# A recurrent kernel on one core: joining copies moved, one filling unit moved, and the last group of steps projected plainly

## The chip, the cores and the metric

The kernel runs on one core of a Trainium2 chip. Its engines are named as in the profile: PE (matrix products), PEld (PE's weight loads), DVE (vector), ACT (scalar, activations and copies), POOL (the general engine) and SP (which here issues DMAs). The metric is the device time of one execution in microseconds; three runs of the kernel before have a median of 1363.82 us (1363.69 to 1363.88).

## The reference

A gated recurrent unit runs over T=128 steps for a batch of 64, with D=H=512, all in 32-bit floats. The output is x plus the sequence of states.

```python
comb = concat([x_t, h]);  z = sigmoid(comb @ Wz + bz);  r = sigmoid(comb @ Wr + br)
h_cand = tanh(concat([x_t, r * h]) @ Wh + bh)
h_new = (1 - z) * h + z * h_cand                  # what is put out, added to x
h_next = tanh(h_new @ Wp + bp) if prop else h_new # prop: every fourth step but the last
```

## The kernel before, in words

**Layout.** The 64 rows of the batch and two halves of the 512 columns make 128 partitions, so h is 128x256. A gate's product (`product`, L196) is four parts k, each two matmuls, one per half (`products`, L184), with 64 columns of stationary operand and 256 of moving one. Every matmul in 32-bit floats is two records in the profile, so a gate is 16 records.

**A step** (the loop from L569) has, in PE's order: the r product with `wh[R]`; the z product; two half turns of rh (`turn`, L205: each is four bf16 transposes on PE and a copy, to `rhT`); the candidate's product, `rc<-wh,rhT`; two half turns of h, the first copied by DVE, the second by ACT; in a step with propagation, also the product with `wp` and two half turns of its tanh. Around it ACT runs the sigmoids of r (L601), the seed of r, the sigmoids of z (L616, L617), the seed of z, tanh (L647) and the seed of the candidate; DVE runs the products and sums (L602, L618, L648, L653). `ORDER` is the order k=0, 2, 1, 3: the first two need only the first half turn.

**The part that comes from x** is worked out ahead, for groups of four steps. The first two groups use `plain` (L411): 12 units of 256 columns a step, with the bias added by DVE into `cp`. From group 2 on, `batches` (L483) does two groups at once by a two-level scheme with seven instead of eight products at each level: 98 units of 192 columns for eight steps. It needs differences of weights, some of them stored in place in `wx` (L316, L324), sums of x made by POOL (`sum_raw12` and so on), and recombinations by POOL into `cp` (`outer_...`). `seed` (L392) copies from `cp` into PSUM what the next step's products add to.

**What sets the order.** Nothing is scheduled by a planner: each engine runs its queue in the order of the program text. The units wait in `queue`; `fill(n)` (L400) puts the next n of them at a place in a step; the copies that read a finished batch (its ends) wait in `pending` until the next `read_out()`. `PLACES` (L537) has, for u = (t-3) mod 8, how many units lie ahead of the candidate, how many behind it, and how many in the propagation. The second number is split over L656, L661 and L663: of 6 units four lie ahead of the first turn of h, one between the turns and one behind the second. The queue for groups 30 and 31 is filled at t=114 and used up in t=122.

**x turned.** From group 4 on POOL splits x in words (`words_x`), a transposing DMA on SP's queue (`planes_x`) turns it, and `join_x` (L268) puts the two planes together on ACT: two copies of 128x512 words in each of the steps with u=5, 6 (even groups) and u=1, 3 (odd ones). They stand at L638, behind the candidate's product and ahead of tanh in ACT's order.

Of the kernel before, what the change touches and what calls it, by code (L numbers as in the profile page):

```python
# [17 lines left out]
def kernel(  # L18
# [29 lines left out]
    nc = tc.nc  # L48
    B, T, D = x.shape
# [6 lines left out]
    Q4 = 4  # L56
    CHUNK = 4
    FIRST = 2
    R, Z, H_ = range(3)
    assert B * S == P and D == H and T % 8 == 0  # L60

# [115 lines left out]
    def idle(n):  # L177
        for _ in range(n):
            nc.tensor.matmul(  # L179
                scratch[0][:B, :], lhsT=zeros[:, :B], rhs=zeros, start=True, stop=True  # L180
            )
# [14 lines left out]
    def product(ps, lT, w, k, start=False):  # L196
        s0, c0 = divmod(k, C)
        products(ps, lT[:, c0, ts(s0, B)], lambda s: w[:, k, ts(s, N)], start)
# [69 lines left out]
    def join_x(g, i):  # L268

        if g * Q4 >= T:  # L270
            return
        new_xT(g)
        nc.scalar.copy(
            xT[g][:, i].bitcast(U16).rearrange("p c (n w) -> p w c n", w=2), xv[g][:, i]
        )
# [62 lines left out]
    def sum_raw12(g):  # L338
        v = xT[g]
        sx[g, 12] = one.tile([P, 4, C, B], F32, tag="s12r", name=f"s12r_{g}")  # L340
        four([sx[g, 12][:, n] for n in range(4)], v[:, 0], v[:, 1])
# [6 lines left out]
    def sum_s12(g):  # L348
        v = xT[g]
        o = sx[g, "o12"] = one.tile([P, 2, 2, P], F32, tag="o12", name=f"o12_{g}")  # L350
        nc.gpsimd.tensor_add(o[:, 0], v[:, 2:4, 0, :], v[:, 2:4, 1, :])
        nc.gpsimd.tensor_sub(o[:, 1], o[:, 0], v[:, 0:2, 0, :])
        s = sx[g, 56] = one.tile([P, 4, 2, B], F32, tag="s56", name=f"s56_{g}")
        four([s[:, n] for n in range(4)], o[:, :, 0], o[:, :, 1])
# [37 lines left out]
    def seed(i, t):  # L392
        if t < T:
            nc.scalar.copy(cut(slots[i]), G[t][:, :, i, :])  # L394
# [5 lines left out]
    def fill(n):  # L400
        for _ in range(min(n, len(queue))):
            unit, end = queue.pop(0)
            unit()
            if end is not None:
                pending.append(end)
# [5 lines left out]
    def plain(t):  # L411
# [20 lines left out]
        ]  # L432
        return [(u, None) for u in units[:-1]] + [(units[-1], end)]

    MB = {}

    def batch(n, ms):

        def region(ps, m):
            return ps[:, m].rearrange("p g u -> p (g u)")  # L440

        def unit(ps, m, j, start):
            g, i = ms[m]
            products(
                region(ps, m), lhs(g, i, j), lambda s: factor(i, j)[:, s], start and m == 0
            )

        def units(ps, j, start):
            return [lambda m=m: unit(ps, m, j, start) for m in range(2)]

        def blocks():
            return MB[n].rearrange("p m b g (a u) -> p m b a g u", a=2)

        def end_1():
            MB[n] = mbp.tile([P, 2, 2, 3, P], F32, tag="mb", name=f"mb_{ms[0][0]}_{ms[0][1]}")
            for m, (g, i) in enumerate(ms):
                M[g, i] = MB[n][:, m]
            T2[n] = one.tile([P, 2, 3, P // 2], F32, tag="cx", name=f"cx_{ms[0][0]}_{ms[0][1]}")
            q1 = one.tile([P, 2, 3, P // 2], F32, tag="cq", name=f"cq_{ms[0][0]}_{ms[0][1]}")
            nc.scalar.copy(T2[n], x_ps)  # L460
            nc.scalar.copy(q1, q_ps)
            nc.vector.tensor_add(T2[n], r_ps, T2[n])  # L462
            nc.vector.tensor_add(blocks()[:, :, 0, 0], a_ps, q1)

        def end_2():
            q2 = one.tile([P, 2, 3, P // 2], F32, tag="cq", name=f"cq2_{ms[0][0]}_{ms[0][1]}")
            nc.scalar.copy(q2, q_ps)  # L467
            nc.vector.tensor_add(blocks()[:, :, 0, 1], r_ps, q2)  # L468
            nc.vector.tensor_add(blocks()[:, :, 1, 0], x_ps, q2)
            nc.vector.tensor_add(blocks()[:, :, 1, 1], q_ps, T2[n])  # L470

        free = units(a_ps, 2, True)
        one_ = units(q_ps, 1, True) + units(r_ps, 5, True) + units(x_ps, 7, True)
        two_ = units(x_ps, 4, False) + units(q_ps, 6, False) + units(r_ps, 3, False)
        seq = [(u, None) for u in free + one_ + two_]
        seq[7] = (seq[7][0], end_1)
        seq[13] = (seq[13][0], end_2)
        return seq

    M = {}  # L480
# [2 lines left out]
    def batches(g):  # L483

        if g * Q4 >= T:
            return []
        ms = [(g, i) for i in (1, 2, 6, 5, 7, 3, 4)] + [(g + 1, i) for i in (1, 6, 2, 5, 3, 7, 4)]
        return sum((batch((g, n), ms[2 * n : 2 * n + 2]) for n in range(7)), [])


    def flat(v):
# [47 lines left out]
    )  # L539


    idle(10)
    spread(0, rc)
    turn_x(0, nc.vector)
# [24 lines left out]
    for t in range(T):  # L569
# [7 lines left out]
        if t < 3:  # L577
            queue.extend(plain(2 * t + 2) + plain(2 * t + 3))
            places = (12, 12)
        elif t == 3:  # L580
            queue.extend(batches(FIRST))
            places = (8, 8, 6)
        elif u == 7:

            queue.extend(batches(even + 2))


        for k in ORDER:
# [1 line left out]
        if t < 6:  # L590
            turn_x((2, 5, 8, 11, 13, 15)[t])
        read_out()
        if u == 0 and pair >= 1:
            outer_u2(odd - 2)
        if t == 3:
            sum_s12(FIRST)
# [3 lines left out]
        for c in range(C):  # L600
            nc.scalar.activation(act_ps[c], slots[R][:, ts(c, P)], AF.Sigmoid)  # L601
            nc.vector.tensor_mul(rh[:, ts(c, P)], act_ps[c], h[:, ts(c, P)])  # L602
        seed(R, t + 1)


        for k in ORDER[: 2 if last else K]:
            product(slots[Z], hT, wh[Z], k)
        rhT = new_T("rhT", f"rhT_{t}")
        for c in range(C):
            turn(rh, rhT, c, f"rhT_{t}", nc.vector)  # L610
        if last:
            for k in ORDER[2:]:
                product(slots[Z], hT, wh[Z], k)
        z = two.tile([P, N], F32, tag="z", name=f"z_{t}")
        keep = two.tile([P, N], F32, tag="keep", name=f"keep_{t}")
        nc.scalar.activation(z, slots[Z], AF.Sigmoid)  # L616
        nc.scalar.activation(slots[Z], slots[Z], AF.Sigmoid, scale=-1.0)  # L617
        nc.vector.tensor_mul(keep, slots[Z], h)  # L618
        seed(Z, t + 1)
        if prop:  # L620
            nc.scalar.copy(cut(slot_p), bias[:, :, 3, :])
# [2 lines left out]
        if t == 0:  # L624
            sum_outer()
            for i in (6, 7, 4):
                sum_inner(i, nc.gpsimd)
                sum_inner_1(i, nc.gpsimd)
        fill(places[0])
        if t < 3:  # L630
            turn_x((3, 6, 9)[t])

# [2 lines left out]
            product(slots[H_], rhT, wh[H_], k)  # L635
        if t != 2:
            read_out()
        if pair >= 0:  # L638
            for n in range(2):
                if u in (5, 6):  # L640
                    join_x(even + 2, 2 * (u - 5) + n)
                elif u in (1, 3) and pair >= 1:
                    join_x(odd, u - 1 + n)
        h_new = two.tile([P, N], F32, tag="h", name=f"h_{t}")
        for c in range(C):
            pc = act_ps[c]
# [4 lines left out]
                nc.vector.tensor_add(o, pc, o)  # L651
                continue
            nc.vector.tensor_add(h_new[:, ts(c, P)], pc, keep[:, ts(c, P)])  # L653
        seed(H_, t + 1)
        read_out()
        fill(places[1] - 3 if places[1] > 6 else 4)  # L656
        h = h_new
        if not last:
            hT = new_T("hT", f"hT_{t}")
            turn(h, hT, 0, f"hT_{t}", nc.vector)  # L660
            fill(1)  # L661
            turn(h, hT, 1, f"hT_{t}", nc.scalar)
        fill(2 if places[1] > 6 else 1)  # L663
        if t == 2:
            sum_outer_1()
        if t == 3:
# [2 lines left out]
        if prop:  # L669
            for k in ORDER:  # L670
                product(slot_p, hT, wp, k)
            read_out()
            h = two.tile([P, N], F32, tag="hprop", name=f"hprop_{t}")
            for c in range(C):
                nc.scalar.activation(h[:, ts(c, P)], slot_p[:, ts(c, P)], AF.Tanh)
            fill(places[2] - 2)
            hT = new_T("hT", f"hpT_{t}")
            for c in range(C):
                turn(h, hT, c, f"hpT_{t}", (nc.vector, nc.scalar)[c])
            fill(2)  # L680
        if t < 5:
            turn_x((4, 7, 10, 12, 14)[t])


        if pair >= 0:
            if u == 0 and pair >= 1:
                outer_c22(odd - 2)
                outer_c21(odd - 2)
            if here:
                if u == 0:  # L690
                    sum_s34(even)
                    outer_1(even)
                elif u == 1:
                    outer_c11(even)
                    sum_raw12(odd)
                elif u == 2:
                    outer_u1(even)
                    outer_5(even)
                    sum_raw4(even)
                elif u == 3:  # L700
                    outer_c12(even)
                    outer_u2(even)
                    outer_c22(even)
                    sum_s12(odd)
                elif u == 4:
                    outer_c21(even)
                    outer_1(odd)
                    sum_s34(odd)
                elif u == 5:
                    outer_u1(odd)  # L710
                    outer_c11(odd)
                    sum_raw4(odd)
                elif u == 7:
                    outer_5(odd)
                    outer_c12(odd)
        if u == 7 and pair >= -1 and (even + 2) * Q4 < T:
# [12 lines left out]
            nc.gpsimd.tensor_add(xr[g][:, j, :], xr[g][:, j, :], h_new)  # L729


        n = 0
        if t >= T - CHUNK:
            n = {T - 2: 3, T - 1: 1}.get(t, 0)
# [60 lines left out]
```

## Time and profile before

| | us |
|---|---|
| median of three runs | 1363.82 |
| profiled execution | 1362.82 |
| its span, first to last instruction | 1361.0 |
| PE busy | 1341.8 |
| POOL busy | 935.7 |
| DVE busy | 686.0 |
| ACT busy | 630.6 |
| from the r product of t=118 (starts 1264.12) to the end | 96.88 |
| from the r product of t=123 (starts 1313.52) to the end | 47.48 |

All rows but the first are from one execution. The granted clock of PE was 0.998 over the span. Ends of matmuls in the trace are modelled, and the two halves of a product overlap, so a sum of busy times says less than the distances between starts. A row of the order in time has its start, its length, the engine, the line, the operation, what it writes and reads, sizes and count; in brackets stands how long the engine sat idle before it, and what ended that. All values of u and t in this document are those of the loop.

### The profile page before, as it was taken

Reading aid. Unit: us, or ns where it says so; the run is one execution under the profiler, and the core shown is the slowest. Engines: PE = TensorE matmul, PEld = TensorE weight load, DVE = VectorE, ACT = ScalarE, POOL = GpSimd, SP = SyncE. Lnnn points to the kernel's source line nnn. Section 1 sums busy time; section 2 is a strip of 40 time slices with the busy share of each in tenths; the row PEclk is TensorE's granted clock in tenths of the full one; section 3 lists DMA queues with packets and bytes.
Section 4 is the critical chain, followed back from the end, with each engine's and each line's share of the span. In section 5 each row is a group of like instructions: output and inputs, shape, how many; then the busy total and the mean of one; then the engine's idle time right before and its main releaser. Section 6 shows DMA issues by size and latency. Waiting matters only on the chain.

```text
span 1361.0 us, 37468 instructions
## 1 busy us (share of the span) xinstructions
PE 1341.8 (99%) x15348; PEld 1033.1 (76%) x15348; DVE 686.0 (50%) x1875; ACT 630.6 (46%) x1857; POOL 935.7 (69%) x1140
## 2 busy tenths in 40 slices
PE   9999999999999999999999999999999999999996
PEld 6877777777777777777777777777777777777764
DVE  3255555555555555555555555555554555555543
ACT  1234544444544544444445444545445445444443
POOL 3448776778667768676787767777676686767740
PEclk9999999999999999999999999999999999999999
DMA  9011223121221222213222221222212212131010
GB/s 287 13 33 34 62 49 78 32 58 39 64 63 33 63 48 48 64 33 78 49 45 52 63 64 33 63 36 60 63 32 64 59 37 63 41 71 33 17 33 16
DMA packets 113572, 73.86 MB, mean 54 GB/s; under 512 B 61556, under 2 KB 109812, under 8 KB 113400
## 3 DMA queue, kind: packets, MB, share of 16 engines
q1 hardware_dynamic: 112336, 69.68, 22.6%
q8 instruction: 121, 1.98, 0.6%
q10 hardware_dynamic: 1064, 1.78, 0.4%
q14 instruction: 51, 0.42, 0.1%
HBM read 39.99 MB, written 16.78 MB: 42 GB/s over the span
## 4 chain that ended last, share of the span: by engine, by line
PE 98%; DVE 1%; ACT 0%; issue 0%; POOL 0%; DVEq 0%; POOLq 0%; ACTq 0%
PE rc L187 33%; PE zp L187 20%; PE scratch_q L187 11%; PE scratch_x L187 11%; PE scratch_r L187 10%; PE scratch_a L187 6%; PE turn L212 6%; PE scratch_q L179 0%; DVE h L653 0%; DVE turn L648 0%; ACT z L616 0%; PE rc L160 0%; ACT turn L647 0%; ACT xT L203 0%; ACT zp L617 0%
## 5 line engine op out<-in xcount | busy, mean ns | idle before, releaser
L187 PE MATMUL rc<-wh,rhT 128*64 128x256 f32 x2048 | 246.6, 381 | 2.0 <-ACT zp L617 2.0
L495 POOL TENSOR_TENSOR cp<-mb,mb 128x768 f32<-128x768 f32 x75 | 136.4, 1819 | 112.8 <-ACT rc L394 67.6
L187 PEld LDWEIGHTS rc<-wh,rhT 128*64 128x64 f32 x2048 | 158.9, 137 | 54.5 <-ACT zp L617 12.4
L187 PE MATMUL rc<-wh,hT 128*64 128x256 f32 x1536 | 183.1, 380 | 0.5 <-DVE hT L203 0.2
L187 PE MATMUL zp<-wh,hT 128*64 128x256 f32 x1536 | 183.2, 379 | 0.0
L203 DVE COPY rhT<-turn 128x256 uint16<-128x256 uint16 x256 | 96.7, 420 | 126.1 <-PE turn L212 126.1
L495 POOL TENSOR_TENSOR cp<-mb 128x768 f32<-128x768 f32 x45 | 81.9, 1819 | 108.2 <-ACT rc L394 107.0
L648 DVE TENSOR_TENSOR turn<-turn,z 128x128 f32<-128x128 f32 x256 | 75.5, 295 | 159.7 <-ACT turn L647 159.7
L187 PEld LDWEIGHTS zp<-wh,hT 128*64 128x64 f32 x1536 | 117.5, 137 | 47.3
L729 POOL TENSOR_TENSOR xr<-xr,h 128x256 f32<-128x256 f32 x127 | 92.8, 731 | 86.2 <-DVE h L653 85.2
L187 PEld LDWEIGHTS rc<-wh,hT 128*64 128x64 f32 x1536 | 111.6, 137 | 44.9 <-issue 1.0
L601 ACT ACTIVATE turn<-rc 128x128 f32<-128x128 f32 x256 | 55.4, 261 | 155.3 <-issue 84.2
L462 DVE TENSOR_TENSOR cx<-scratch_r,cx 128x384 f32<-128x384 f32 x105 | 58.6, 558 | 128.3 <-ACT cx L460 128.3
L203 ACT COPY hT<-turn 128x256 uint16<-128x256 uint16 x127 | 47.3, 373 | 155.8 <-PE turn L212 96.6
L495 POOL TENSOR_TENSOR mb<-mb,mb 128x768 f32<-128x768 f32 x60 | 109.4, 1824 | 14.2 <-DVE mb L470 14.2
L468 DVE TENSOR_TENSOR mb<-scratch_r,cq 128x384 f32<-128x384 f32 x105 | 58.6, 558 | 91.0 <-ACT cq L467 91.0
L394 ACT COPY rc<-cp 128x256 f32<-128x256 f32 x254 | 95.6, 376 | 11.6 <-POOL s L335 0.4
L616 ACT ACTIVATE z<-zp 128x256 f32<-128x256 f32 x128 | 49.2, 384 | 102.7 <-PE zp L187 100.8
L647 ACT ACTIVATE turn<-rc 128x128 f32<-128x128 f32 x256 | 56.7, 261 | 76.2 <-PE rc L187 76.2
L212 PEld LDWEIGHTS <-h 128*64 128x64 bf16 x1016 | 47.7, 109 | 50.5 <-DVE h L653 45.7
L394 ACT COPY zp<-cp 128x256 f32<-128x256 f32 x127 | 47.8, 377 | 74.5 <-DVE keep L618 74.5
L212 PE MATMUL turn<-ident,h 128*64 128x128 bf16 x1016 | 76.7, 227 | 5.4 <-DVE h L653 5.4
(152 smaller groups left out, 2960.4 us busy)
## 6 DMA issues: line engine op xcount, KB each, us to landing
xr<-in_x_dram SPq DMA_DIRECT2D x62, 256.0 KB, 4.2
out_dram<-xr SPq DMA_DIRECT2D x62, 256.0 KB, 3.4
xs<-in_x_dram SPq DMA_DIRECT2D x56, 256.0 KB, 4.3
wh<-in_L_cond_Wr_dram SPq DMA_DIRECT2D x2, 512.0 KB, 7.5
wh<-in_L_cond_Wz_dram SPq DMA_DIRECT2D x2, 512.0 KB, 8.9
wh<-in_L_cond_Wh_dram SPq DMA_DIRECT2D x2, 512.0 KB, 11.4
early<-in_x_dram SPq DMA_DIRECT2D x4, 256.0 KB, 13.4
wp<-in_L_cond_Wp_dram SPq DMA_DIRECT2D x1, 1024.0 KB
```

Source lines behind the costliest of these rows:

```text
L187: nc.tensor.matmul(ps[s * B : (s + 1) * B], lhsT=lhs, rhs=rhs(s), start=start, stop=True, skip_group_check=True,)
L203: (eng.copy if eng is nc.scalar else eng.tensor_copy)(dst, src)
L212: nc.tensor.transpose(pt[s * B : (s + 1) * B, w, :], words.rearrange("p (n w) -> p w n", w=2)[:, w, :], ident16,)
L394: nc.scalar.copy(cut(slots[i]), G[t][:, :, i, :])
L462: nc.vector.tensor_add(T2[n], r_ps, T2[n])
L468: nc.vector.tensor_add(blocks()[:, :, 0, 1], r_ps, q2)
L495: nc.gpsimd.tensor_add(dst, a, b)
L601: nc.scalar.activation(act_ps[c], slots[R][:, ts(c, P)], AF.Sigmoid)
L616: nc.scalar.activation(z, slots[Z], AF.Sigmoid)
L647: nc.scalar.activation(pc, slots[H_][:, ts(c, P)], AF.Tanh)
L648: nc.vector.tensor_mul(pc, pc, z[:, ts(c, P)])
L729: nc.gpsimd.tensor_add(xr[g][:, j, :], xr[g][:, j, :], h_new)
```

## The change

- The two joining copies of a step are issued one behind the seed of r and one behind the sigmoids of z and `keep`, ahead of the seed of z.
- Where six units lie behind the candidate, four lie ahead of the first turn of h, two between the turns and none behind the second. Where eight lie there, the split stays five, one and two. In the first three steps (twelve) it is five, one, six instead of nine, one, two.
- The last group (31) is projected plainly. The queue filled at t=114 has only the 49 units of group 30; seven are left for t=118. At t=118 nine DMAs on SP's queue load k=1, 0 and 2 of `wx` again (k=3 was never changed in place). `plain_last` puts 48 units of 256 columns into the queue at t=119: the three gates of k=3 for t=124 and 125 first, then the rest.
- The last nine steps are thin: no units ahead of the candidate; z's product is split, two parts before the first half turn of rh, one after each; `TAIL` gives the units ahead of, between and behind the turns of h, and in the propagation. The seed of the candidate for the last step moves into that step.

```diff
+    def plain_last():
...
+        t0 = LAST * Q4
+        seq = [(u, None) for t in (t0, t0 + 1) for u in units(t, (R, Z, H_), (3,))]
+        for t in (t0, t0 + 1):
+            us = units(t, (R, Z, H_), (1, 0, 2))
+            seq += [(u, None) for u in us[:-1]] + [(us[-1], lambda t=t: end(t, (R, Z, H_)))]
+        for t, gates in ((t0 + 2, (R, Z, H_)), (t0 + 3, (R, Z)), (t0 + 3, (H_,))):
+            us = units(t, gates, (3, 1, 0, 2))
+            seq += [(u, None) for u in us[:-1]] + [(us[-1], lambda t=t, g=gates: end(t, g))]
+        return seq
...
+    def reload():
...
+        for k in (1, 0, 2):
+            for i in range(3):
+                load_w(wx[:, :, i, :], gates_in[i], k, k + 1, nc.sync)
...
+    TAIL = (
+        ((4, 1, 0), (2, 1)), ((4, 1, 0), ()), ((4, 1, 0), ()), ((4, 1, 0), ()),
+        ((4, 1, 0), (2, 1)), ((4, 1, 0), ()), ((5, 1, 2), ()), ((3, 1, 0), ()), ((0, 0, 0), ()),
+    )
...
+        thin = t >= T - 9
+        if thin:
...
+            places, behind = TAIL[t - (T - 9)]
+            if t == T - 9:
+                assert not queue
+                queue.extend(plain_last())
+        if t == T - 10:
...
+            places = (4, 6)
...
+        def join(n):
+            if pair >= 0 and u in (5, 6):
+                join_x(even + 2, 2 * (u - 5) + n)
+            elif pair >= 1 and u in (1, 3):
+                join_x(odd, u - 1 + n)
...
         seed(R, t + 1)
-
-
-        for k in ORDER[: 2 if last else K]:
+        join(0)
+
+
+        for k in ORDER[: 2 if thin else K]:
             product(slots[Z], hT, wh[Z], k)
...
             turn(rh, rhT, c, f"rhT_{t}", nc.vector)
-        if last:
-            for k in ORDER[2:]:
-                product(slots[Z], hT, wh[Z], k)
+            if thin:
+                product(slots[Z], hT, wh[Z], ORDER[2 + c])
...
         nc.vector.tensor_mul(keep, slots[Z], h)
+        join(1)
         seed(Z, t + 1)
...
-        fill(places[0])
+        if not thin:
+            fill(places[0])
...
-        fill(places[1] - 3 if places[1] > 6 else 4)
+        fill(places[0] if thin else 5 if places[1] > 6 else 4)
...
-            fill(1)
+            fill(places[1] if thin else 1 if places[1] > 6 else 2)
             turn(h, hT, 1, f"hT_{t}", nc.scalar)
-        fill(2 if places[1] > 6 else 1)
+        fill(places[2] if thin else places[1] - 6)
```

More of the change, by code (lines that the diff above doesn't have):

```diff
@@ L58 @@
     FIRST = 2
+    LAST = T // Q4 - 1
     R, Z, H_ = range(3)
@@ L433, in plain, with units, end @@
         return [(u, None) for u in units[:-1]] + [(units[-1], end)]
+    def plain_last():
+        def units(t, gates, first_k):
+            first, second = scratch[:2] if t % 2 == 0 else scratch[2:]
+            regions = (first[:, :N], first[:, N:], second[:, :N])
+            return [
+                lambda e=e, k=k: product(
+                    regions[e], xT[LAST][:, t % Q4], wx[:, :, e, :], k, k == 3 and e != Z
+                )
+                for k in first_k
+                for e in gates
+            ]
+        def end(t, gates):
+            first, second = scratch[:2] if t % 2 == 0 else scratch[2:]
+            new_cp(t // 2)
+            if R in gates:
+                nc.vector.tensor_add(
+                    G[t][:, :, 0:2, :],
+                    first.rearrange("p (g c n) -> p c g n", g=2, c=C),
+                    bias[:, :, 0:2, :],
+                )
+            if H_ in gates:
+                nc.vector.tensor_add(
+                    G[t][:, :, 2, :], cut(second[:, :N]), bias[:, :, 2, :]
+                )
+        t0 = LAST * Q4
[11 more added lines that the diff above has]
+                load_w(wx[:, :, i, :], gates_in[i], k, k + 1, nc.sync)
     MB = {}
@@ L448, in units @@
         def units(ps, j, start):
-            return [lambda m=m: unit(ps, m, j, start) for m in range(2)]
+            return [lambda m=m: unit(ps, m, j, start) for m in range(len(ms))]
         def blocks():
@@ L457, in end_1 @@
                 M[g, i] = MB[n][:, m]
+            nm = len(ms)
             T2[n] = one.tile([P, 2, 3, P // 2], F32, tag="cx", name=f"cx_{ms[0][0]}_{ms[0][1]}")
             q1 = one.tile([P, 2, 3, P // 2], F32, tag="cq", name=f"cq_{ms[0][0]}_{ms[0][1]}")
[L460 to L463, printed above, removed]
+            nc.scalar.copy(T2[n][:, :nm], x_ps[:, :nm])
+            nc.scalar.copy(q1[:, :nm], q_ps[:, :nm])
+            nc.vector.tensor_add(T2[n][:, :nm], r_ps[:, :nm], T2[n][:, :nm])
+            nc.vector.tensor_add(blocks()[:, :nm, 0, 0], a_ps[:, :nm], q1[:, :nm])
         def end_2():
             q2 = one.tile([P, 2, 3, P // 2], F32, tag="cq", name=f"cq2_{ms[0][0]}_{ms[0][1]}")
[L467 to L470, printed above, removed]
+            nm = len(ms)
+            nc.scalar.copy(q2[:, :nm], q_ps[:, :nm])
+            nc.vector.tensor_add(blocks()[:, :nm, 0, 1], r_ps[:, :nm], q2[:, :nm])
+            nc.vector.tensor_add(blocks()[:, :nm, 1, 0], x_ps[:, :nm], q2[:, :nm])
+            nc.vector.tensor_add(blocks()[:, :nm, 1, 1], q_ps[:, :nm], T2[n][:, :nm])
         free = units(a_ps, 2, True)
@@ L475, in batch @@
         seq = [(u, None) for u in free + one_ + two_]
-        seq[7] = (seq[7][0], end_1)
-        seq[13] = (seq[13][0], end_2)
+        for n_units, end in ((4 * len(ms), end_1), (7 * len(ms), end_2)):
+            seq[n_units - 1] = (seq[n_units - 1][0], end)
         return seq
@@ L486, in batches @@
             return []
-        ms = [(g, i) for i in (1, 2, 6, 5, 7, 3, 4)] + [(g + 1, i) for i in (1, 6, 2, 5, 3, 7, 4)]
-        return sum((batch((g, n), ms[2 * n : 2 * n + 2]) for n in range(7)), [])
+        ms = [(g, i) for i in (1, 2, 6, 5, 7, 3, 4)]
+        if g + 1 < LAST:
+            ms += [(g + 1, i) for i in (1, 6, 2, 5, 3, 7, 4)]
+        return sum((batch((g, n), ms[2 * n : 2 * n + 2]) for n in range(7) if 2 * n < len(ms)), [])
     def flat(v):
@@ L538 @@
         (6, 8, 6), (2, 6), (6, 6), (2, 6), (6, 8, 6), (2, 6), (2, 6), (6, 8),
+    )
+    TAIL = (
+        ((4, 1, 0), (2, 1)), ((4, 1, 0), ()), ((4, 1, 0), ()), ((4, 1, 0), ()),
+        ((4, 1, 0), (2, 1)), ((4, 1, 0), ()), ((5, 1, 2), ()), ((3, 1, 0), ()), ((0, 0, 0), ()),
     )
@@ L585 @@
             queue.extend(batches(even + 2))
+        thin = t >= T - 9
[6 more added lines that the diff above has]
+            places = (4, 6)
+            assert len(queue) == 7
+        def join(n):
[3 more added lines that the diff above has]
+                join_x(odd, u - 1 + n)
         for k in ORDER:
@@ L592 @@
         read_out()
-        if u == 0 and pair >= 1:
+        if t == T - 1:
+            seed(H_, t)
+        if u == 0 and pair >= 1 and odd - 2 < LAST:
             outer_u2(odd - 2)
@@ L637 @@
             read_out()
[L638 to L643, printed above, removed]
         h_new = two.tile([P, N], F32, tag="h", name=f"h_{t}")
@@ L653 @@
             nc.vector.tensor_add(h_new[:, ts(c, P)], pc, keep[:, ts(c, P)])
-        seed(H_, t + 1)
+        if t < T - 2:
+            seed(H_, t + 1)
         read_out()
-        fill(places[1] - 3 if places[1] > 6 else 4)
+        fill(places[0] if thin else 5 if places[1] > 6 else 4)
         h = h_new
@@ L675 @@
                 nc.scalar.activation(h[:, ts(c, P)], slot_p[:, ts(c, P)], AF.Tanh)
-            fill(places[2] - 2)
+            fill(behind[0] if thin else places[2] - 2)
             hT = new_T("hT", f"hpT_{t}")
@@ L679 @@
                 turn(h, hT, c, f"hpT_{t}", (nc.vector, nc.scalar)[c])
-            fill(2)
+            fill(behind[1] if thin else 2)
         if t < 5:
@@ L685 @@
         if pair >= 0:
-            if u == 0 and pair >= 1:
+            if u == 0 and pair >= 1 and odd - 2 < LAST:
                 outer_c22(odd - 2)
@@ L694 @@
                     outer_c11(even)
-                    sum_raw12(odd)
+                    if odd < LAST:
+                        sum_raw12(odd)
                 elif u == 2:
@@ L703 @@
                     outer_c22(even)
-                    sum_s12(odd)
+                    if odd < LAST:
+                        sum_s12(odd)
                 elif u == 4:
                     outer_c21(even)
-                    outer_1(odd)
-                    sum_s34(odd)
-                elif u == 5:
+                    if odd < LAST:
+                        outer_1(odd)
+                        sum_s34(odd)
+                elif u == 5 and odd < LAST:
                     outer_u1(odd)
@@ L712 @@
                     sum_raw4(odd)
-                elif u == 7:
+                elif u == 7 and odd < LAST:
                     outer_5(odd)
@@ L729 @@
             nc.gpsimd.tensor_add(xr[g][:, j, :], xr[g][:, j, :], h_new)
+        if t == T - 10:
+            reload()
         n = 0
```

## The prediction

> **What bounds the kernel now.** I read the page's busy shares first, then the windows of a few stages, then the order in time of single steps.
>
> ```profile
> PE 1341.8 (99%) x15348; PEld 1033.1 (76%) x15348; DVE 686.0 (50%) x1875; ACT 630.6 (46%) x1857; POOL 935.7 (69%) x1140
> PE   9999999999999999999999999999999999999996
> ```
>
> Columns of the windows: stretch, its length, then the busy time and instructions of PE, its weight loads, DVE, ACT and POOL.
>
> ```profile
> 605.09:613.65 8.56, 8.56 (x100) 6.28 (x99) 4.48 (x13) 4.63 (x14) 7.77 (x11) 1.00 0.09 18
> 1295.19:1303.63 8.44, 8.44 (x100) 6.32 (x98) 4.02 (x12) 3.84 (x13) 2.98 (x7) 1.00 0.09 18
> 1313.52:1361.00 47.48, 34.03 (x336) 23.26 (x336) 16.64 (x53) 15.43 (x52) 9.10 (x9) 0.98 0.10 23
> ```
>
> TensorE sets the time up to 1313 us. The first two windows are one step each (from the first r product to that of the next step) with the same matrix work, eight units of filling. Both read as fully busy, yet one takes 0.12 us longer: a busy share hides waits shorter than the tail of a matmul, so I count distances between starts. The last window is different: the queue of units is empty from step 123 on, and 47.48 - 34.03 = 13.45 us are open waiting.
>
> Prices on PE, from starts in the trace: a product of four k (a gate) 1.73 us, so a unit of 256 columns is 0.43; a unit of 192 columns is 0.325; half a turn 0.11, and 0.03 more after a wait.
>
> The step of 605.09 (t=54, with joins), the one of 1295.19 (t=121, without), and an empty one (t=125):
>
> ```profile
> 609.44 1.95 PE L187 MATMUL rc<-wh,rhT 128*64 128x256 f32 x16
> 610.30 1.40 ACT L273 COPY xT<-xv 128x512 uint16<-128x512 uint16 x2
> 611.57 0.45 ACT L647 ACTIVATE turn<-rc 128x128 f32<-128x128 f32 x2
> 612.65 0.31 PE L212 MATMUL turn<-ident,h 128*64 128x128 bf16 x4
> ...
> 1299.55 1.95 PE L187 MATMUL rc<-wh,rhT 128*64 128x256 f32 x16
> 1301.59 0.43 ACT L647 ACTIVATE turn<-rc 128x128 f32<-128x128 f32 x2 [1.12 <-PE rc L187]
> 1302.63 0.31 PE L212 MATMUL turn<-ident,h 128*64 128x128 bf16 x4
> 1303.17 0.31 PE L212 MATMUL turn<-ident,h 128*64 128x128 bf16 x4
> ...
> 1337.88 1.95 PE L187 MATMUL rc<-wh,rhT 128*64 128x256 f32 x16 [0.50 <-ACT zp L617]
> 1340.96 0.31 PE L212 MATMUL turn<-ident,h 128*64 128x128 bf16 x4 [1.14 <-DVE h L653]
> 1341.36 0.41 DVE L203 COPY hT<-turn 128x256 uint16<-128x256 uint16 x1
> 1341.92 1.95 PE L187 MATMUL rc<-wh,hT 128*64 128x256 f32 x16
> ```
>
> From the candidate's product to the first turn of h takes 3.08 us where nothing is in the way (1299.55 to 1302.63, 1337.88 to 1340.96), but 3.21 with two joins ahead of tanh on ACT. Four units (1.30) behind the product (1.73) cover 3.03 of it. From the first turn of h to the next r product takes 0.96 when only the chain sets it (1340.96 to 1341.92).
>
> **The change, part by part. Joins.** They cost ACT 0.76 us each either way. In t=54 they run from 610.30 to 611.70 and tanh starts 2.13 us after the product instead of 2.04. Starts of r give the price in PE time: the joined steps at u=3, 5, 6, 1 (t=54, 56, 57, 60) take 8.56, 8.54, 8.56, 8.48; the same eight units without joins (t=120, 121) take 8.44. That is 0.12 + 0.10 + 0.12 + 0.04 = 0.38 in eight steps. There are 56 such steps, 14 of each kind (t=8 to 118): 14 x 0.38 = 5.3 us. The new places: the first join follows the seed of r. In t=54 that seed ends at 607.92 and ACT stood idle 0.84 until z at 608.76; 0.76 fits. The second follows both sigmoids of z (end 609.42) and ends at about 610.2, 1.4 us ahead of tanh. Queued behind it on ACT are the seed of z, free to start only at 609.99 anyway (after keep), so 0.2 later and wanted by the next step's z product 5 us on, and then tanh. Were the gap too short, z and keep would move, and keep (ended 609.95) is wanted at 612.30 by the sum of h: 2.3 us of cover, more than a join, so a loss is excluded. Their transposing DMAs land 4.6 us after issue, issued a full step or more before. No gain 0, whole gain 5.3; I take 5.3, since the steps without joins show it directly.
>
> **The moved unit.** In the steps whose second place is 6 (u=1, 2, 3, 5, 6; 72 of them from t=4 to 117) the six units lie four, turn, two, turn, none, instead of four, one, one. Today from first turn to r: 0.11 + 0.03 + 0.325 + 0.07 wait for h + 0.11 + 0.03 + 0.325 = 1.00 (1302.63 to 1303.63). After: 0.14 + 0.65 + 0.11 = 0.90, so the chain's 0.96 decides, and the r product restarts after a wait, which in the empty steps makes it 1.75 instead of 1.73 (1333.48 to 1335.23). 0.96 + 0.025 against 1.00 saves 0.015: 72 x 0.015 = 1.1 us. The second half of hT now comes 0.25 later, at 0.79 + 0.35 + 0.37 + 0.15 = 1.66 (turn, gap, ACT copy, gap to PE), wanted at 0.96 + 0.86 = 1.82: hidden by 0.16. Bounds: 2.9 gained if nothing waits, 1 lost if the restart costs the 0.05 that it once shows (t=124, 1325.04 to 1326.82).
>
> **The last group plain.** Removed: 49 units of 0.325 = 15.9 us, with their readings on ACT and DVE and sums on POOL (no releaser of a PE wait there). Added: 48 of 0.43 = 20.7 us. The Trainium skill, Perfetto Trace Analysis, section Identifying the Most-Contended Engine, says to look for the engine of highest occupancy and spend the effort on unloading that one. PE at 99% is that engine, and this part loads it: by the rule the tail grows by 4.8 us and the whole change comes to 1363.8 + 4.8 - 6.4 = 1362.2. But the rows above place 13.45 us of waiting behind the last unit, and the plain units are held back to be laid there. I go by the rows, step by step from the r product of t=118 (1264.12; 96.88 us to the end):
>
> - t=118: seven units are left, three behind the candidate. 1.73 + 1.73 + 0.22 + 1.30 = 4.98, then 3.08 and 0.96: 9.02 (8.55 before).
> - A thin step (120 to 122, 124): the first turn of rh comes 2.68 after r starts (1350.35 to 1353.03 in the last step, whose split of z is like it), then 0.14 + 0.43 + 0.11 + 0.43: the candidate at 3.79. It takes 1.73, four units 1.73 (more than the 1.35 that the chain needs), then 0.96: 8.20. The one unit between the turns lies inside the 0.96.
> - t=119 and 123, with the propagation: as thin to 8.20, product 1.75, two units 0.86 (tanh and turn come 2.31 after the product's start, 1321.89 to 1324.20, hidden), then turn to r 0.84: 11.65. The copy for the propagation puts ACT 0.1 to 0.2 behind for tanh; the units' 0.38 over the chain cover that.
> - t=125: eight units, none waiting: 9.19. t=126: 3.79 + 3.08 + 0.96 = 7.83. t=127: 10.65 before, 0.09 less as the candidate starts at 3.79 instead of 3.88: 10.56.
>
> Sum 9.02 + 2 x 11.65 + 4 x 8.20 + 9.19 + 7.83 + 10.56 = 92.70: 4.2 us saved. The additions of the bias into cp (0.68 and 0.41 on DVE in the first steps) come at the head of a step, with DVE's products for rh 2.3 us away and only a hT copy before them; the seed of h in the last step waits for one of them and sits ahead of the r sigmoid, ready about 0.9 us into r's 1.73. Bounds: 0 (the chain stretches with the units) to 6.
>
> **The reload.** Nine loads of 256 KB on SP's queue. They wait for PE's last read of wx in t=118, some 7.8 us into it; queued behind them on SP are only the output of the group before and later loads, with several steps of room. The seventh plain unit is the first that needs one, 1.4 + 8.20 + 1.75 + 0.43 = about 11.6 us after issue; the fifteenth needs the last load 27 us after. A lone 256 KB load lands in 4.2 us; 2.36 MB at the 287 GB/s of the page's first slice are 8.2. I take 12.4 for the last and 6.9 for the third: hidden. The upper bound is the rival below.
>
> **Sum.** 5.3 + 1.1 + 4.2 = 10.6 us. The profiled execution took 1362.82 (span 1361.0, 1.82 around it), so 1352.2 there; the median of the runs is 1.00 higher, 1363.82, so 1353.2.
>
> **Rivals.** (1) The joins' price only moves: something else on ACT or DVE holds tanh as late, and only the other parts pay: 1363.8 - 5.3 = 1358.5. For it: only 0.08 of slack behind the first join. Against: t=120 and 121 without joins, and 1.4 us of ACT before tanh. 12%. (2) The plain group pays nothing, its work as large as the holes it fills: 1357.4. For it: the rule above; against: 13.45 us of holes. 10%. (3) Slower: the reload. If the nine loads land one after another at the 5.6 us that the first 512 KB load of wx took, the last comes at 50 us, 23 after the fifteenth unit wants it: 1353.2 + 23 = 1376. It decides from the ninth load landing 27 + 10.6 = 38 us after the first issue, 4.2 us apiece. Against: the first slice of the page moved 287 GB/s with the same kind of load. 4%. (4) The change doesn't do what it says: a hidden wait eats the shift and the joins' gain, and the time stays within 0.2%: 4%. My forecast has 70%, with 1350.5 to 1356.5 of its own.
>
> A difference under 0.2% (2.7 us) can't be told from none by this measurement. Faster gathers the forecast, (1) and (2): 0.92; same 0.04; slower 0.04. The range takes in the forecast's bounds and (1) and (2): 1349.5 to 1358.5.
>
> **What would show it.** Joins: the steps at u=1, 3, 5, 6 last 8.42 to 8.44, joins lie in ACT's gaps ahead of z and of the seed of z, tanh 2.04 after the candidate. Unit: 0.96 to 0.99 from first turn to r. Tail: from the r product of t=118 to the end 92.7; thin steps 8.20, the waits for h gone. Reload: no PE wait for a load in t=119 to 121. I am wrong if joined steps stay above 8.5, if thin steps exceed 8.4, or if PE waits on a DMA.

## The result, and the profile after

The changed kernel takes 1353.89 us (median of six runs, 1352.5 to 1355.61) against 1363.82: a ratio of 0.9929, 95% interval 0.9916 to 0.9942. The prediction was 1353.2. The profiled execution took 1353.16, with a span of 1351.3.

The windows of the tail, before and after, from the r product of t=118 to the end (columns as in the prediction: stretch, length, busy time of PE, PEld, DVE, ACT, POOL; behind them the granted clock, the DMA share and GB/s):

```profile
1264.12:1361.00 96.88, 83.26 (x908) 61.29 (x904) 42.27 (x124) 37.90 (x120) 39.10 (x42) 0.99 0.10 23
```

```profile
1258.45:1351.30 92.85, 86.66 (x906) 59.31 (x900) 39.71 (x117) 33.70 (x111) 14.75 (x15) 0.99 0.14 40
```

PE is busy 3.40 us longer and the stretch is 4.03 us shorter: the waiting fell from 13.62 to 6.19. A thin step of the changed kernel, t=121, in order of time (rows left out are marked):

```profile
1287.14 1.95 PE L188 MATMUL rc<-wh,hT 128*64 128x256 f32 x16
...
1289.81 0.31 PE L213 MATMUL turn<-ident,rh 128*64 128x128 bf16 x4
...
1290.93 1.90 PE L188 MATMUL rc<-wh,rhT 128*64 128x256 f32 x16
...
1294.38 0.28 PE L213 MATMUL turn<-ident,h 128*64 128x128 bf16 x4
...
1294.71 0.42 DVE L204 COPY hT<-turn 128x256 uint16<-128x256 uint16 x1 [0.26 <-PE turn L213]
...
1295.28 0.44 PE L188 MATMUL rc<-wh,hT 128*64 128x256 f32 x2
```

The turn of rh comes 2.67 after r (2.68 said), the candidate 3.79 after it (3.79), the turn of h 3.45 after that, r 0.90 later: 8.14 (8.20 said). PE's rows in this listing name no wait, yet 0.24 us of the last distance are one (0.90 less 0.11 + 0.44 + 0.11: a half turn, a unit, a half turn).

A step with joins, t=105 (u=6), on PE and then on ACT:

```profile
1125.57 1.95 PE L188 MATMUL rc<-wh,hT 128*64 128x256 f32 x16
...
1129.97 1.95 PE L188 MATMUL rc<-wh,rhT 128*64 128x256 f32 x16
...
1133.06 0.31 PE L213 MATMUL turn<-ident,h 128*64 128x128 bf16 x4
...
1133.85 0.28 PE L213 MATMUL turn<-ident,h 128*64 128x128 bf16 x4
1134.01 0.44 PE L188 MATMUL rc<-wh,hT 128*64 128x256 f32 x2
```

```profile
1128.12 0.38 ACT L395 COPY rc<-cp 128x256 f32<-128x256 f32 x1
1128.44 0.77 ACT L274 COPY xT<-xv 128x512 uint16<-128x512 uint16 x1
1129.28 0.39 ACT L690 ACTIVATE z<-zp 128x256 f32<-128x256 f32 x1
1129.56 0.38 ACT L691 ACTIVATE zp<-zp 128x256 f32<-128x256 f32 x1
1129.87 0.76 ACT L274 COPY xT<-xv 128x512 uint16<-128x512 uint16 x1
1130.52 0.38 ACT L395 COPY zp<-cp 128x256 f32<-128x256 f32 x1
1132.01 0.43 ACT L717 ACTIVATE turn<-rc 128x128 f32<-128x128 f32 x2 [1.11 <-PE rc L188]
```

The joins lie in the two gaps, z starts as soon as its product allows (3.71 after r, as in this kernel's steps without joins), and ACT sits idle 1.11 us before tanh, which now comes 2.04 after the candidate (2.13 in t=54 before). The step lasts 8.44.

Set against each other, the two profiles differ by 9.7 us of span: 0.69 lost before t=6, 6.36 gained from t=6 to t=117, 4.03 gained in the tail.

### The profile page after: what moved, and what is told of

Same layout as the page of the kernel before. It is cut to its first block, busy times and chain, and to the rows that moved or that the text cites. A ratio compares the mean times of both kernels' runs of the same rounds, so it can differ in the third digit from the quotient of the medians.

```text
span 1351.3 us, 37427 instructions
## 1 busy us (share of the span) xinstructions
PE 1339.2 (99%) x15344; PEld 1114.8 (82%) x15344; DVE 679.8 (50%) x1868; ACT 628.2 (46%) x1848; POOL 910.1 (67%) x1111
## 4 chain that ended last, share of the span: by engine, by line
PE 98%; DVE 1%; ACT 0%; issue 0%; POOL 0%; DVEq 0%; ACTq 0%; POOLq 0%
PE rc L188 34%; PE zp L188 20%; PE scratch_q L188 11%; PE scratch_x L188 11%; PE scratch_r L188 10%; PE scratch_a L188 6%; PE turn L213 5%; PE scratch_q L180 0%; PE zp L161 0%; ACT xT L204 0%; DVE rh L676 0%; PE rc L161 0%; DVE mb L516 0%; DVE mb L517 0%; DVE turn L718 0%
## 5 line engine op out<-in xcount | busy, mean ns | idle before, releaser
L188 PEld LDWEIGHTS rc<-wh,rhT 128*64 128x64 f32 x2048 | 167.3, 137 | 45.2 <-ACT zp L691 9.3
L544 POOL TENSOR_TENSOR cp<-mb,mb 128x768 f32<-128x768 f32 x72 | 130.9, 1818 | 103.2 <-ACT rc L395 61.1
L188 PE MATMUL rc<-wh,hT 128*64 128x256 f32 x1536 | 186.6, 383 | 0.5
L188 PE MATMUL zp<-wh,hT 128*64 128x256 f32 x1536 | 186.9, 379 | 0.0
L188 PEld LDWEIGHTS zp<-wh,hT 128*64 128x64 f32 x1536 | 130.4, 137 | 31.4
L188 PEld LDWEIGHTS rc<-wh,hT 128*64 128x64 f32 x1536 | 123.0, 136 | 27.0 <-issue 1.3
L544 POOL TENSOR_TENSOR mb<-mb,mb 128x768 f32<-128x768 f32 x58 | 105.7, 1822 | 12.5 <-DVE mb L517 12.5
L274 ACT COPY xT<-xv 128x512 uint16<-128x512 uint16 x112 | 85.7, 765 | 0.0
L723 DVE TENSOR_TENSOR h<-turn,keep 128x128 f32<-128x128 f32 x254 | 74.1, 292 | 15.4
L213 PEld LDWEIGHTS <-h 128*64 128x64 bf16 x1016 | 59.7, 110 | 22.2 <-DVE h L723 12.3
```

The lines of the kernel that those rows point to most:

```text
L188: nc.tensor.matmul(ps[s * B : (s + 1) * B], lhsT=lhs, rhs=rhs(s), start=start, stop=True, skip_group_check=True,)
L213: nc.tensor.transpose(pt[s * B : (s + 1) * B, w, :], words.rearrange("p (n w) -> p w n", w=2)[:, w, :], ident16,)
L274: nc.scalar.copy(xT[g][:, i].bitcast(U16).rearrange("p c (n w) -> p w c n", w=2), xv[g][:, i])
L544: nc.gpsimd.tensor_add(dst, a, b)
```

## The experiments

The theory was that three parts add up: joins 5.3 us, moved unit 1.1, tail 4.2. The rivals: the joined steps gain from the moved unit; the plain group costs its matrix work; the price only moves to another engine; the reload costs time. Every kernel below was profiled once. The three right columns are distances between starts of r products in its trace, worked out by me: where t=6 starts, from there to t=118, and from t=118 to the end of the span. The parts of a step are so steady that these distances repeat within 0.2 us, while whole runs do not.

| kernel | median us | ratio, 95% interval | r of t=6 at | t=6 to 118 | t=118 to end |
|---|---|---|---|---|---|
| before | 1363.82 | | 110.90 | 1153.22 | 96.88 |
| changed | 1353.89 | 0.9916 to 0.9942 | 111.59 | 1146.86 | 92.85 |
| e1 joins alone | 1357.12 | 0.9939 to 0.9964 | 110.57 | 1147.07 | 96.77 |
| e2 unit alone | 1363.89 | 0.9994 to 1.0012 | 111.75 | 1153.16 | 96.99 |
| e3 tail alone | 1359.94 | 0.9957 to 0.9980 | 111.89 | 1153.30 | 92.80 |
| e4 changed again | 1353.99 | 0.9918 to 0.9943 | 112.26 | 1146.92 | 92.92 |
| e5 no reload | 1354.77 | 0.9916 to 0.9946 | 113.90 | 1147.01 | 92.98 |
| e6 both joins behind r | 1353.92 (one run) | | 112.19 | 1147.01 | 92.90 |
| e7 plain units early | 1358.18 | 0.9940 to 0.9970 | 112.15 | 1147.01 | 97.14 |
| e8 three tail edits | 1350.68 | 0.9891 to 0.9925 | 110.90 | 1146.90 | 90.89 |
| e9 two tail edits | 1351.85 | 0.9902 to 0.9929 | 111.03 | 1146.76 | 91.31 |
| e10 unit at u=1, 5 | 1352.18 | 0.9900 to 0.9927 | 112.33 | 1146.81 | 91.26 |

**Joins alone.** The kernel before with

```diff
+        def join(n):
...
         seed(R, t + 1)
+        join(0)
...
         nc.vector.tensor_mul(keep, slots[Z], h)
+        join(1)
         seed(Z, t + 1)
...
-        if pair >= 0:
-            for n in range(2):
...
```

> The kernel before with the joining copies alone moved (one behind the seed of r, one behind the sigmoids of z). My theory: the joins ahead of tanh were the whole extra wait of the joined steps, so these steps fall to the 8.44 us of the steps without joins (by 0.12, 0.10, 0.12 and 0.04 at u=3, 5, 6, 1), 5.3 us in all: about 1358.5. Rival, that the moved unit earns what the joined steps gained: these steps stay at 8.55 and the time stays within 1 us of 1363.8.

Steps at u=3, 5, 6 fell to 8.44 as said, u=1 to 8.37, from 8.48. That is 6.15 us from t=6 to 118, 0.85 more than expected, all of it from u=1: the baseline of 8.44 from two steps of u=5 and 6 was not that of u=1. The first turn of h in u=1 now waits for nothing, where the other kinds still wait 0.04 and restart 0.03 later; why its chain is shorter by these hundredths was not found out. The rival, that the moved unit earns this, fell.

**The moved unit alone.** The kernel before with

```diff
-        fill(places[1] - 3 if places[1] > 6 else 4)
+        fill(5 if places[1] > 6 else 4)
...
-            fill(1)
+            fill(1 if places[1] > 6 else 2)
...
-        fill(2 if places[1] > 6 else 1)
+        fill(places[1] - 6)
```

> The kernel before with the moved unit alone (four, two and none round the turns of h, and the split of the first three steps that goes with it). My theory: from the first turn of h to the next r product 1.00 us becomes 0.97 or 0.98, 0.015 in 72 steps, 1.1 us at most: 1362.7 to 1363.8; the steps with u=2, which lost only 0.003 in the changed kernel, say nearer to 1363.8. Rival: the unit closes the wait ahead of the second turn, and the joined steps fall to 8.44: about 1358.5.

Nothing: 0.06 us from t=6 to 118, and 0.2 lost in t=4 and 5 (10.08 and 11.17 against 9.85 and 11.21; why was not found out). The PE rows of this kernel round the end of t=54 show where it went:

```profile
613.49 0.31 PE L212 MATMUL turn<-ident,h 128*64 128x128 bf16 x4
613.62 0.50 PE L187 MATMUL scratch_x<-tt,s4r 128*64 128x192 f32 x4
613.95 0.49 PE L187 MATMUL scratch_x<-tt,s12r 128*64 128x192 f32 x4
614.28 0.28 PE L212 MATMUL turn<-ident,h 128*64 128x128 bf16 x4
614.44 1.95 PE L187 MATMUL rc<-wh,hT 128*64 128x256 f32 x16
616.19 1.06 PE L187 MATMUL zp<-wh,hT 128*64 128x256 f32 x8
```

The wait ahead of the second turn is gone. In its place r waits 0.05 for the first half of hT (614.28 + 0.11 = 614.39), comes 0.95 after the first turn, and its product takes 1.75 instead of 1.73.

**The tail alone.** The changed kernel with the joins and the split as before:

```diff
-        join(0)
...
-        join(1)
...
+        join(0)
+        join(1)
         h_new = two.tile([P, N], F32, tag="h", name=f"h_{t}")
...
-        fill(places[0] if thin else 5 if places[1] > 6 else 4)
+        fill(places[0] if thin else places[1] - 3 if places[1] > 6 else 4)
...
-            fill(places[1] if thin else 1 if places[1] > 6 else 2)
+            fill(places[1] if thin else 1)
...
-        fill(places[2] if thin else places[1] - 6)
+        fill(places[2] if thin else 2 if places[1] > 6 else 1)
```

> The changed kernel with the joining copies and the split of the units as before: the last group plain, thin last steps and the reload alone. My theory: all up to t=117 lasts as before, and from the r product of t=118 to the end 92.7 to 92.9 us instead of 96.9: about 1359.7. Rival, that the plain group costs its added matrix work: 1368; rival, that it pays only with the other parts: 1363.8.

4.08 us less behind t=118 and nothing before it. The three parts alone make 6.15, 0.06 and 4.08; together, from t=6 to the end, 10.39 (1250.10 less 1239.71). They add up.

**The changed kernel again**, without an edit.

> The changed kernel once more, unchanged. My theory: steps as in its first profile within 0.02 us; the runs spread over 3 us because the start differs, so the spans differ ahead of t=6 and not behind it. Rival: a wait in the steps comes and goes from run to run, so that step lengths differ between the two profiles. Theory for the two late turns of rh: the one in t=127 comes again (the seed of the candidate stands ahead of the r sigmoid), the one in t=124 may not. Time 1352 to 1356.

As the theory had it: 1146.92 and 92.92 against 1146.86 and 92.85, but the r product of t=6 starts 0.67 later. The kernel before ran between 1362.65 and 1365.55 in the 16 runs beside these. The start is told of at the end.

**Without the reload.** This kernel leaves `reload()` out.

```diff
-        if t == T - 10:
-            reload()
```

> The changed kernel without the nine loads that bring back k=1, 0 and 2 of wx, so that the last group is projected with weights that still hold differences. My theory: the loads were hidden, from the r product of t=118 to the end 92.8 to 92.9 us as with them, time 1352.5 to 1355.5. Rival, that the reload costs time (a wait of PE, or the DMAs in the way of others): half a microsecond or more less behind t=118.

92.98 against 92.85 and 92.92: the reload costs nothing. The changed kernel's issues on SP's queue show that it even starts earlier than I said, in t=117 and not 7.8 us into t=118 (1258.45):

```profile
1254.01 0.37 SPq L99 DMA_DIRECT2D wx<-in_L_cond_Wr_dram  x1
...
1257.74 0.53 SPq L99 DMA_DIRECT2D wx<-in_L_cond_Wh_dram  x1
```

The last seven units read `tw` and `tt`, not `wx`, so nothing holds the loads until they are done.

**Both joins behind the seed of r.**

```diff
         join(0)
+        join(1)
...
-        join(1)
```

> The changed kernel with both joining copies behind the seed of r. My theory: the sigmoids of z and keep come about 0.65 us later, and PE does not notice, since keep is wanted over 2 us on: steps at u=1, 3, 5, 6 stay at 8.33, 8.44, 8.42, 8.44. Rival (the price only moves on ACT and DVE): these steps grow by some tenths, up to 0.65.

ACT in t=105 of this kernel:

```profile
1129.16 1.40 ACT L274 COPY xT<-xv 128x512 uint16<-128x512 uint16 x2
1130.43 0.37 ACT L691 ACTIVATE z<-zp 128x256 f32<-128x256 f32 x1
...
1132.74 0.43 ACT L717 ACTIVATE turn<-rc 128x128 f32<-128x128 f32 x2 [0.80 <-PE rc L188]
```

z starts 4.13 us after r (1126.30) instead of 3.71 in the changed kernel, tanh 6.44 after r in both, and the steps last 8.33, 8.44, 8.42 and 8.44. The cover of z and keep is real: a z that starts 0.42 later costs nothing, while the two copies right ahead of tanh did.

**The plain units early.** Same instructions, another `TAIL`:

```diff
+        ((4, 1, 0), (2, 1)), ((4, 1, 1), ()), ((4, 2, 3), ()), ((5, 2, 5), ()),
+        ((5, 2, 2), (2, 2)), ((0, 0, 0), ()), ((0, 0, 0), ()), ((0, 0, 0), ()), ((0, 0, 0), ()),
```

> The changed kernel with the same 48 plain units laid earlier: none in t=124 to 126, and 8, 6, 9, 12 and 13 in t=119 to 123. Same instructions, other places. My theory: a unit costs 0.43 us where PE has nothing to wait for and next to nothing where it would wait for h, so t=121 to 123 grow by 1.4, 2.7 and 1.6 us, t=124 to 126 shrink to about 7.8 each, together about 4 us more than the changed kernel: 1357.5 to 1358. Rival (the sum of the matrix work decides, wherever it lies): within 1 us of the changed kernel.

97.14, 4.3 us more than the changed kernel and as long as the tail before. A window that holds the starts of r in t=123 to 126 of this kernel shows the waits back (34.60 us, of which PE is busy 31.47):

```profile
1305.40:1340.00 34.60, 31.47 (x328) 20.64 (x324) 13.52 (x39) 10.91 (x37) 2.68 (x4) 1.00 0.07 17
```

Steps 121 to 123 grew by 1.45, 2.74 and 1.69; 125 and 126, now empty, last 7.79. A plain unit costs about its 0.43 where PE has no hole (three more in t=122 than in 121 make 1.30 us), and little where it has one (t=126 of the changed kernel holds four and lasts 7.75). With its units laid early the whole edit of the tail earns nothing. The empty steps show one thing more: they lasted 8.43 and 8.44 in the kernel before, with the candidate 4.40 after r (1333.48 to 1337.88 in t=125) instead of 3.79. So the thin order, with z's product split, is worth 0.65 us in a step without units, and the tail's gain is not that of filled holes alone. The split was not run without the plain group.

**Tail edits.** Three on top of the changed kernel, then the same without the one to `places` (t=118):

```diff
+        ((3, 2, 0), (2, 1)), ((3, 2, 0), ()), ((3, 2, 0), ()), ((3, 2, 0), ()),
+        ((3, 2, 0), (2, 1)), ((3, 2, 0), ()), ((5, 1, 2), ()), ((3, 1, 0), ()), ((0, 0, 0), ()),
...
-            places = (4, 6)
+            places = (2, 6)
...
-        if t == T - 1:
-            seed(H_, t)
...
         seed(R, t + 1)
+        if last:
+            seed(H_, t)
```

> The changed kernel with three edits in its tail: in t=118 two of the seven units ahead of the candidate; in t=119 to 124 three units ahead of the first turn of h and two between the turns; and the seed of the candidate for the last step behind the sigmoids of r instead of ahead. My theory: t=118 falls from 8.95 to about 8.40, the six thin steps by 0.16 each (the chain's 3.08 from candidate to turn instead of 3.45, against 1.11 instead of 0.89 to r), and the turn of rh in t=127 comes 0.40 earlier: 1.9 us less, from the r product of t=118 to the end about 91.0, time near 1352. Rival for t=127, that something else than the seed's place holds the sigmoid: no change there.

> The changed kernel with two of the three tail edits: three units ahead of the first turn of h and two between the turns in t=119 to 124, and the seed of the candidate for the last step behind the sigmoids of r; t=118 as in the changed kernel. My theory: t=118 back at 8.95, the thin steps at 7.92 to 7.97 and 11.4 to 11.5, t=127 to the end 10.56: from the r product of t=118 to the end 91.1 us, 91.4 if the odd wait of about 0.3 comes in one of them: 1.5 to 1.8 us below the changed kernel. Rival: the gain of the version with three edits came from t=118: less than 1 us.

90.89 and 91.31. In the first, units of t=118 add to sums that have not been read yet: ACT's copy from `scratch_x` starts at 1266.45, behind the three units (from 1264.60 on) that it stood ahead of. So its gain at t=118 (8.44 instead of 8.95) is not to be had this way. The second leaves t=118 as it was and is 1.5 to 1.6 us below the changed kernel's tail: thin steps of 7.91 to 7.97 (8.24 in t=124, which has a wait told of below), 11.42 with propagation, 10.54 in the last. Its median, 1351.85, is the lowest but for e8; its interval against before overlaps with that of the changed kernel, so the step lengths carry this gain, not the medians.

**The moved unit at u=1 and 5 only**, on top of that:

```diff
-            fill(places[1] if thin else 1 if places[1] > 6 else 2)
+            fill(places[1] if thin else 2 if u in (1, 5) else 1)
...
-        fill(places[2] if thin else places[1] - 6)
+        fill(places[2] if thin else places[1] - 6 if places[1] > 6 else 0 if u in (1, 5) else 1)
```

> The version before this one with the moved unit kept only at u=1 and u=5, and four, one and one as in the kernel before at u=2, 3 and 6. My theory: the restart of r behind a wait is carried as 0.02 us into the next step, so u=0, 4 and 7 fall back to 14.30, 14.09 and 10.18, u=1 and 5 stay at 8.33 and 8.42, the others at 8.44 and 9.67 to 9.69: 0.5 to 0.9 us less from t=6 to t=118 than with the unit moved everywhere (1146.9). Rival: the 0.02 comes from elsewhere: no difference over 0.2 us.

My theory fell. u=0, 4 and 7 did come back by 0.02 each and u=5 to 8.39, but u=2 and u=6 grew by 0.04: 1146.81 against 1146.76. The hundredths behind a restarted r (one that had to wait for h) are moved, not saved.

## Why the prediction was right

- **Joins, 5.3 said, 6.15 measured.** Mechanism right: the copies ahead of tanh were the joined steps' extra wait, and both gaps hold. The mis-sized term is u=1, 0.04 a step said and 0.11 measured, since its own step without joins was not in the trace.
- **Moved unit, 1.1 said, about 0 measured.** The step that failed is "0.96 + 0.025 against 1.00 saves 0.015". The row for the chain was right (0.95), so the chain did take over, and a moved step ends 0.04 earlier. The mis-sized term is the restart, 0.025 said. In a step that follows a moved one (t=57 in e2) r takes 1.75 instead of 1.73, and the candidate, 4.40 after r instead of 4.35, is 0.02 later once more: 0.04 in all, as much as was gained. The steps with eight units, which end no earlier, pay 0.02 outright (u=0, 4, 7 from 14.30, 14.09, 10.18 to 14.32, 14.11, 10.21). Only u=1 and 5, which follow unmoved steps, keep something (0.04 and 0.02), and t=4 and 5 lose 0.2 between them. u=4 and 7 pay in their r product. u=0 follows a step whose split was not changed, and its r takes 1.73; the z products of t=59, before and in e2, show that the 0.02 was carried into it:

```profile
656.74 1.90 PE L187 MATMUL zp<-wh,hT 128*64 128x256 f32 x16
658.68 0.39 ACT L616 ACTIVATE z<-zp 128x256 f32<-128x256 f32 x1 [0.50 <-PE zp L187]
...
665.20 1.91 PE L187 MATMUL zp<-wp,hT 128*64 128x256 f32 x16
667.09 0.55 PE L187 MATMUL scratch_q<-tw,o 128*64 128x192 f32 x4
```

```profile
657.55 1.93 PE L187 MATMUL zp<-wh,hT 128*64 128x256 f32 x16
659.51 0.38 ACT L616 ACTIVATE z<-zp 128x256 f32<-128x256 f32 x1 [0.50 <-PE zp L187]
...
666.00 1.93 PE L187 MATMUL zp<-wp,hT 128*64 128x256 f32 x16
667.92 0.55 PE L187 MATMUL scratch_q<-tw,o 128*64 128x192 f32 x4
```

  Starts on PE are as before up to the product with `wp`, but z comes 1.96 after its product's start instead of 1.94, and the unit behind the product with `wp` 1.92 instead of 1.89. In e10, where u=6 is not moved, z comes after 1.94 again. What makes the carry was not settled.
- **Tail, 4.2 said, 4.0 to 4.1 measured.** Thin steps 8.14 to 8.15 (8.20), with propagation 11.58 (11.65), t=118 8.95 (9.02), t=125 9.20 (9.19), t=126 7.75 (7.83). Two terms were missed. In t=127 I had the seed of the candidate "ready about 0.9 us into r's 1.73"; it waited for the whole r product, and stood ahead of the sigmoids:

```profile
1342.42 0.38 ACT L395 COPY rc<-cp 128x256 f32<-128x256 f32 x1 [1.71 <-PE rc L188]
1342.83 0.43 ACT L675 ACTIVATE turn<-rc 128x128 f32<-128x128 f32 x2
1343.13 0.49 DVE L676 TENSOR_TENSOR rh<-turn,h 128x128 f32<-128x128 f32 x2 [2.47 <-ACT turn L675]
```

  The sigmoid starts 2.43 after r (1340.40) instead of 2.03 (t=121). With the seed behind it (e9) the last step falls from 10.90 to 10.54: shown. Both slots lie in one tile of PSUM, which may be why the copy waits for the other slot's product; that was not tried. The other is t=124, 8.43 against 8.20 said: its r sigmoid starts 2.32 after r instead of 2.03. This wait comes again in e4, e3, e5, e6, e7, e9 and e10, while e8 has none at t=124 and one of 0.35 in t=122, on DVE ahead of the sum of h. Its cause stays open.
- **The rule and the rows.** The rule of loading the busiest engine less, taken from the Trainium skill (Perfetto Trace Analysis, section Identifying the Most-Contended Engine), would have had the tail grow by 4.8; it shrank by 4.0. The section says more than the prediction took from it: for TensorE the busy share of matmuls is not a good measure of how close it is to its limit, and the busy share of weight loads is named as one of two better ones. That share was 76% here, against 99%. e7 shows where the added matrix work does count: with the same units where PE has no hole, the tail takes 97.14.
- **The rivals.** (1) fell with e1 and e6, (2) with e3, (3) with e5, (4) with the result. From t=6 to the end 10.39 us were gained, 10.6 said. That the sum was nearer than its terms is luck: 0.85 too little for the joins and 1.1 too much for the unit cancel.

## What to carry to other kernels

On a chain that one engine covers with filling work, a copy costs not its length but what it puts off: find the gap in its engine's queue that ends before the next chain operation, and count starts, since busy shares of 100% hid 0.12 us a step here. Extra work on the busiest engine is free where it fills a hole, and near full price a few steps earlier, so hold it back for the stretch that has nothing else to run. Closing one small wait can hand its time to the next; take a step without the suspect, of the same kind, as baseline.

## What the runs showed of the hardware

In the profiled executions the spread of 3 us comes from the first 24 us. The r product of t=0 starts at 22.81 (e1), 23.15 (before), 23.64 (changed), 24.31 (e4) and 25.95 (e5), and the distances behind t=6 repeat. Windows from 10 to 24 us, of before and of e5 (the column behind POOL is the granted clock):

```profile
10.00:24.00 14.00, 14.00 (x118) 10.89 (x116) 2.66 (x7) 0.00 (x0) 8.17 (x9) 0.88 1.07 355
```

```profile
10.00:24.00 14.00, 14.00 (x96) 9.23 (x94) 2.89 (x7) 0.00 (x0) 8.28 (x9) 1.00 1.07 352
```

PE did 96 records instead of 118 in the same time in e5, at a recorded clock of 1.00: its first products start 1.5 us later (12.06 against 10.51) and take 0.63 us a record until about 17.5 us, those of before only until 13.5, and 0.38 behind that. The mean recorded clock of the profiles is 0.998 or 0.999 where t=0 starts by 23.2, 0.997 from 23.6 to 24.4, and 1.0 in e5, where it starts last: the record of the clock does not show this slow phase where it is longest. What makes the phase longer or shorter was not tried.
